# A graph attention layer: blocks of adj fetched in pairs, and fewer, larger transfers of x and of the results

## The chip, the cores and the metric

The kernel runs on one core of a Trainium2 chip. The metric is device time in microseconds (us) of one execution. Before the change it is 235.88 us, the median of three runs from 235.42 to 236.04. A core has five engines that run beside each other, each in its own program order: TensorE (PE, matmuls), VectorE (DVE), ScalarE (ACT), GpSimd (POOL) and SyncE (SP, which here only issues transfers). Sixteen DMA engines move data between the chip's memory (HBM) and the on-chip buffer (SBUF), 128 partitions wide.

## The reference

The layer takes x (4096 x 512), an additive mask adj (4096 x 4096), weights W (512 x 2048, four heads of 512) and vectors a, all f32:

```
ht  = (x @ W) per head                        # 4 heads, 4096 x 512
e   = leaky_relu(src[:, None] + dst[None, :], 0.01) + adj
att = softmax(e, axis=-1)
out = layernorm(x + mean over heads of (att @ ht))
```

The entries of adj go up to 1e9, while src and dst are small. So in nearly every row the softmax is 1 at the largest entry of adj and 0 elsewhere. The result of row i is then layernorm(x[i] + x[c] @ mean of W over heads), with c the column of the largest entry of adj[i].

## The kernel before

The kernel computes that short form, bounds for each row whether the lead of its largest entry is big enough, and runs a general path (`general`) for blocks of rows where it is not. The general path is not entered with these inputs.

The 4096 rows are worked on in 32 blocks of 128 rows; row p*32 + b stands in partition p of block b. So the same partition of two neighbouring blocks holds two neighbouring rows of adj. A block of adj is 2 MB, 16 KB in each partition. It lies in one of six buffers (`adj_pool`, AHEAD + 1). `hold` has room for all of x and becomes the result in place; its upper half first holds W.

The order on each engine is written out by hand. The loop over t = 0 to 31 (lines 423 to 477) does, at step t:

- SP issues the load of block t + 5 (`load_adj`, L122). It waits until DVE is through with block t - 1, which had the buffer. Before it, at t = 3, 7, 11, 15 and 19, SP issues x for four blocks (`load_x`, L125; 1 MB), at t = 26 x for the last four. Blocks 0 and 31 are fetched in four pieces, blocks 28 to 30 in two. SP has eight semaphores for its transfers, used in turn, so that at most eight are under way.
- DVE reduces block t to the maxima of segments (`segment_maxima`, L169): 16 entries each up to block 17, 32 from then on. It does it in two halves. Between them stands `find_column(t - 2)`: the second largest entry of the fetched segment (L208) and the place of the largest (L214). After both halves `find_segment(t)` finds the largest segment (L176, L178).
- POOL, in this order: adds up the column of block t - 2 (L216), issues the gather of the 128 rows of x that belong to it (`gather_rows`, `y`, L202), at even steps computes 1/sd for blocks t - 6 and t - 5 (`rstd`, L271 to L273), and for block t adds up the row of the segment (L185) and issues its fetch from adj (`lead`, `lead_early`, L191). Both gathers are indirect transfers, on another queue than SP's.
- PE transposes y of block t - 3 (`turn`, L229), adds x by a product with the identity (`residual`, L237) and multiplies with the mean of W (`products`, L244). Up to t = 14 it also turns W and forms vectors for the bound (L350, L358).
- ACT copies the transposed y (L231), takes the statistics of block t - 4 (`stats`, L266, L268), the norm of x (L251), and at even steps writes the normalised blocks t - 6 and t - 5 into `hold` (`finish`, L277).

From block 24 on (BEHIND) the sums are put aside into a buffer of adj (`put_by`) and finished in the tail, and x of those blocks is loaded at the last step. After the loop SP stores the results of blocks 0 to 23, blocks 0 to 7 in two transfers of four blocks, the others by two (`store`, L329). The tail (lines 486 to 542) looks for the column of the last block over the whole row (L222), gathers, multiplies and normalises the last blocks and stores them.

Of the kernel before, what the change touches and what calls it, by code (L numbers as in the profile page):

```python
# [9 lines left out]
F32 = mybir.dt.float32  # L10
# [10 lines left out]
P = 128  # L21
# [47 lines left out]
def leading_rows(ctx, tc, x, adj, W, a, out, ident, v, n_bad, any_bad):  # L69
# [8 lines left out]
    nc = tc.nc  # L78
    N, D = x.shape
    H = a.shape[0]  # L80
    KB, NB, S = D // P, N // P, N // E
    S_EARLY = N // E_EARLY
    AHEAD = 5
    Q = 4
    PIECES = 4
    LATE = NB - Q
    BEHIND = LATE - Q

    once = ctx.enter_context(tc.tile_pool(name="once", bufs=1))
    adj_pool = ctx.enter_context(tc.tile_pool(name="adj_pool", bufs=AHEAD + 1))  # L90
    y_pool = ctx.enter_context(tc.tile_pool(name="y_pool", bufs=4))
    lead_pool = ctx.enter_context(tc.tile_pool(name="lead_pool", bufs=2 * Q + 1))
    small = ctx.enter_context(tc.tile_pool(name="small", bufs=5))
    rows = ctx.enter_context(tc.tile_pool(name="rows", bufs=2))
    psum = ctx.enter_context(tc.tile_pool(name="psum", bufs=4, space=bass.MemoryType.PSUM))

    adj_rows = adj.rearrange("(p nb) m -> nb p m", nb=NB)
    adj_segs = adj.rearrange("n (s e) -> (n s) e", e=E)
    adj_segs_early = adj.rearrange("n (s e) -> (n s) e", e=E_EARLY)
    x_rows = x.rearrange("(p nb) d -> p nb d", nb=NB)  # L100
# [7 lines left out]
    w_sum = once.tile([P, KB, D], F32, name="w_sum")  # L108
    a_rows = once.tile([2 * H, D], F32, name="a_rows")

    once.tile([P, 32], F32, name="pad_end")
    adj_t = {}

    def pieces(ib):
        return PIECES if ib in (0, NB - 1) else 2 if ib >= LATE else 1

    def load_adj(ib):
        if 0 <= ib < NB:
            t = adj_t[ib] = adj_pool.tile([P, N], F32, name="adj_t")
            n = pieces(ib)  # L120
            for k in range(n):
                nc.sync.dma_start(t[:, ts(k, N // n)], adj_rows[ib][:, ts(k, N // n)])  # L122

    def load_x(lo, n):
        nc.sync.dma_start(hold[:, ds(lo, n), :], x_rows[:, ds(lo, n), :])  # L125
# [7 lines left out]
    for kb in range(KB):  # L133
        load_w(kb)
        load_adj(kb + 1)
    load_x(0, Q)
    for ib in range(KB + 1, AHEAD):
        load_adj(ib)

    make_identity(nc, ident)  # L140
    first = once.tile([P, NB], U32, name="first")
# [18 lines left out]
    seg_of, at_of, lead_of, y_t, yt_of, o_ps = {}, {}, {}, {}, {}, {}  # L160

    def segment_maxima(ib, lo, hi):

        e = E_EARLY if ib < EARLY else E
        if lo == 0:
            seg_of[ib] = small.tile([P, N // e], F32, name=f"seg{e}", bufs=2)
        n = max(pieces(ib), 2)
        for k in range(lo * n // PIECES, hi * n // PIECES):
            nc.vector.tensor_reduce(  # L169
                seg_of[ib][:, ts(k, N // e // n)],  # L170
                adj_t[ib][:, ts(k, N // n)].rearrange("p (s e) -> p s e", e=e), axis=AX.X, op=OP.max,
            )

    def find_segment(ib):
        seg = seg_of.pop(ib)
        nc.vector.max(out=top[:, ib, :], in_=seg)  # L176
        at = at_of[ib] = small.tile([P, 8], U32, name="at")
        nc.vector.max_index(at, top[:, ib, :], seg)  # L178
        if ib < NB - 1:
            fetch_segment(ib)  # L180
# [29 lines left out]
    def find_column(ib):  # L210
        if ib < BEHIND:
            find_inner(ib)
        within = small.tile([P, 8], U32, name="within")
        nc.vector.max_index(within, top[:, ib, :], lead_of[ib])  # L214
        col = small.tile([P, 1], U32, name="col")
        nc.gpsimd.tensor_tensor(col, at_of.pop(ib), within[:, 0:1], op=OP.add)  # L216
        gather_rows(ib, col)
# [31 lines left out]
    def row_norm(ib):  # L249
        sq = rows.tile([P, D], F32, name="sq")  # L250
        nc.scalar.activation(sq, hold[:, ib, :], AF.Square, accum_out=xx[:, ib : ib + 1])  # L251

    def put_by(ib):

        if ib == BEHIND:
            o_ps["by"] = adj_pool.tile([P, N // D, D], F32, name="adj_t")
        nc.scalar.copy(o_ps["by"][:, ib - BEHIND, :], o_ps.pop(ib))

    def add_x(engine, ib):
        o = o_ps[ib] = o_ps["by"][:, ib - BEHIND, :]  # L260
        engine.tensor_add(o, o, hold[:, ib, :])
# [8 lines left out]
    def rstd(i):  # L270
        nc.gpsimd.tensor_scalar(sd[:, i], sd[:, i], 1.0 / D, EPS, op0=OP.mult, op1=OP.add)  # L271
        nc.gpsimd.tensor_tensor(sd[:, i], sd[:, i], power[:, : i.stop - i.start], op=OP.pow)  # L272
        nc.gpsimd.tensor_mul(nm[:, i], nm[:, i], sd[:, i])  # L273
# [54 lines left out]
    def store(queue, lo, n):  # L328
        queue.dma_start(out_rows[:, ds(lo, n), :], hold[:, ds(lo, n), :])  # L329

    def mean_of_heads(kb):
        o = psum.tile([P, D], F32, name="o")
        for h in range(H):
            nc.tensor.matmul(o, ident, hold[:, w_at + kb * H + h, :], start=(h == 0), stop=(h == H - 1))  # L334
        nc.scalar.activation(w_sum[:, kb, :], o, AF.Copy, scale=1.0 / H)  # L335
# [5 lines left out]
    def turn_a():  # L341
        tp = psum.tile([P, KB, P], F32, name="tp", bufs=2)
        for k in range(KB):
            nc.tensor.transpose(tp[:, k, : 2 * H], a_rows[:, ts(k, P)], ident[: 2 * H, : 2 * H])
        nc.scalar.copy(at_d, tp[:, :, : 2 * H])

    def turn_w(kb, h):
        tp = psum.tile([P, KB, P], F32, name="tp", bufs=2)
        for k in range(KB):
            nc.tensor.transpose(tp[:, k, :], hold[:, w_at + kb * H + h, ts(k, P)], ident)  # L350
        wt = rows.tile([P, KB, P], F32, name="wt")
        nc.scalar.copy(wt, tp)  # L352
        return wt
# [9 lines left out]
    def head_norms():  # L363
        nc.vector.tensor_copy(v, pv)
        vv = once.tile([P, KB, 2 * H], F32, name="vv")
        nc.vector.tensor_mul(vv, v, v)
        pn = psum.tile([P, KB, 2 * H], F32, name="px", bufs=1)
        nc.tensor.matmul(pn, ones, vv, start=True, stop=True)
        n2 = once.tile([P, 2 * H], F32, name="n2")
        nc.vector.tensor_reduce(n2, pn.rearrange("p k c -> p c k"), axis=AX.X, op=OP.add)  # L370
        nc.scalar.activation(n2, n2, AF.Sqrt)
        both = once.tile([P, H], F32, name="both")
        nc.vector.tensor_add(both, n2[:, :H], n2[:, H:])
        nc.vector.tensor_reduce(vn, both, axis=AX.X, op=OP.max)
# [40 lines left out]
        nc.vector.tensor_reduce(total, pg, axis=AX.X, op=OP.add)  # L415
        nc.vector.tensor_scalar(any_bad, total, -1.0, float(N), op0=OP.mult, op1=OP.add)

    x_at = {lo - 1: (lo, Q) for lo in range(Q, BEHIND, Q)}
    vectors = [(kb, h) for kb in range(KB) for h in range(H)]
    vectors_at = {t: 2 if t < 3 else 1 for t in range(1, 15)}  # L420
    COLUMN, PROJECT, STATS, FINISH = 2, 3, 4, 6
# [1 line left out]
    for t in range(NB):  # L423
        if t == NB // 2:
            tc.mark_branch_hint_location("general", engines=HINTED)
        if t in x_at:
            load_x(*x_at[t])
        if t + AHEAD == NB - 1:
            load_x(LATE, Q)
        load_adj(t + AHEAD)  # L430
        middle = 1 if t == NB - 1 else 2
        segment_maxima(t, 0, middle)
        if t >= COLUMN:
            find_column(t - COLUMN)
        segment_maxima(t, middle, PIECES)
        pair = FINISH <= t < BEHIND + FINISH and t % 2 == 0
        if pair:
            rstd(slice(t - FINISH, t - FINISH + 2))
        if t == NB - 1:
            for ib in (BEHIND, BEHIND + 2):  # L440
                load_x(ib, 2)
        find_segment(t)
        if t < 2:
            mean_of_heads(t)
        elif t == 2:
            mean_of_heads(2)
            mean_of_heads(3)
        if t == 0:
            turn_a()
        turned = [(*vectors[0], turn_w(*vectors.pop(0))) for _ in range(vectors_at.get(t, 0))]  # L450
        if t == 16:
            head_norms()
        ib = t - PROJECT
        if t == NB - 1:
            for late in range(LATE, NB):
                row_norm(late)
        if t == NB - 2:
            residual(LATE)
            residual(LATE + 1)
        if ib >= 0:  # L460
            turn(ib)
            if ib > BEHIND:
                products(ib - 1, KB - 1, KB)
            if ib < BEHIND:
                residual(ib)
        for some in turned:
            head_vector(*some)
        if ib >= 0:
            products(ib, 0, KB if ib < BEHIND else KB - 1)
        if t >= BEHIND + STATS:  # L470
            put_by(t - STATS)
        elif t >= STATS:
            stats(t - STATS)
            row_norm(t - STATS)
        if pair:
            finish(t - FINISH)
            finish(t - FINISH + 1)
# [3 lines left out]
    nc.scalar.activation(xx, xx, AF.Sqrt)  # L481
    for ib in range(0, 2 * Q, Q):
        store(nc.sync, ib, Q)
    for ib in range(2 * Q, BEHIND, 2):
        store(nc.sync, ib, 2)
    add_x(nc.gpsimd, BEHIND)
    find_column(NB - 2)
    fetch_segment(NB - 1)
# [207 lines left out]
```

## Time and profile before

| what | value |
|---|---|
| median of three runs | 235.88 us |
| the profiled execution's own time | 236.22 us |
| its span, first to last instruction | 234.7 us |
| DVE busy | 192.2 us, 82% |
| PE busy | 200.7 us, 86% |
| ACT busy | 111.7 us, 48% |
| POOL busy | 100.7 us, 43% |
| moved by DMA | 97.06 MB, mean 414 GB/s |
| largest group: segment maxima, DVE L169 | 145.9 us in 68 |
| DVE idle before L169, released by the landing of adj | 29.4 us |
| mean granted PE clock | 0.959 |

The page divides the span into 40 slices of 5.87 us and gives the busy share of each engine in tenths. "DMA" is the mean share of the 16 DMA engines. Queue q1 carries SP's transfers, q0 the gathers. In the timeline each row has start, duration, engine, line, operation, output and input tile, and in brackets how long the engine was idle before it and what ended the wait. The page also has a chain, which follows the last work back to what released it; its share for the landing of adj is 42%.

### The profile page before, as it was taken

How to read it: one execution, taken by the hardware profiler on the slowest of the kernel's cores; microseconds unless marked ns; L12 is line 12 of the kernel's file. 1: busy time of each engine (PE TensorE's matmuls, PEld its weight loads, DVE VectorE, ACT ScalarE, POOL GpSimd, SP SyncE). 2: the span in 40 equal slices, each digit the busy share in tenths (PEclk: the TensorE clock that was granted, in tenths of full speed). 3: DMA queues.
4: the chain of work that ended last, by engine and by line, in shares of the span. 5: the costliest groups of instructions: out<-in, count | busy, mean ns of one | idle time of the engine just before them, and what ended most of it. 6: DMA issues, size and time to landing. Idle time of an engine off the chain costs nothing.

```text
span 234.7 us, 2494 instructions
## 1 busy us (share of the span) xinstructions
PE 200.7 (86%) x683; PEld 103.0 (44%) x683; DVE 192.2 (82%) x302; ACT 111.7 (48%) x267; POOL 100.7 (43%) x212
## 2 busy tenths in 40 slices
PE   0099859999999999999969979789987988999980
PEld 0034514765656555555525424244433442444360
DVE  2726975669969996999689998998699999989871
ACT  2002112255574647474747464646464555187561
POOL 2022142414626463546444555564364554457400
PEclk9999877999999999999997999979997999999998
DMA  6999999999999999999999999999999999999994
GB/s 233 423 409 430 431 429 415 430 426 425 431 431 421 426 428 428 438 418 436 421 437 431 419 434 422 434 417 435 422 436 413 422 426 423 413 425 420 414 374 197
DMA packets 13697, 97.06 MB, mean 414 GB/s; under 512 B 2152, under 2 KB 2664, under 8 KB 7792
## 3 DMA queue, kind: packets, MB, share of 16 engines
q1 hardware_dynamic: 10080, 88.08, 89.0%
q0 software_dynamic: 3584, 8.77, 9.5%
q8 instruction: 6, 0.10, 0.2%
q14 instruction: 11, 0.09, 0.1%
q10 hardware_dynamic: 16, 0.02, 0.0%
HBM read 88.47 MB, written 8.39 MB: 413 GB/s over the span
## 4 chain that ended last, share of the span: by engine, by line
DMA 48%; POOL 19%; issue 17%; DVE 11%; PE 2%; ACT 0%; POOLq 0%; SPq 0%; DVEq 0%
DMA adj_t<-in_adj_dram 42%; DVE seg L169 8%; POOL y L202 6%; POOL lead L191 5%; DMA y<-in_x_dram,col 3%; DMA lead<-in_adj_dram,row 2%; POOL sd L272 2%; PE o L286 2%; DVE col L222 1%; POOL row L185 1%; POOL start L198 1%; POOL col L216 1%; POOL lead_early L191 1%; DVE at L178 1%; DVE top L176 1%
## 5 line engine op out<-in xcount | busy, mean ns | idle before, releaser
L169 DVE TENSOR_REDUCE seg<-adj_t 128x128 f32<-128x2048 f32 (+3 forms) x68 | 145.9, 2148 | 29.5 <-DMA adj_t<-in_adj_dram 29.4
L244 PE MATMUL o<-w_sum,yt 128*128 128x512 f32 x248 | 116.8, 612 | 0.7 <-ACT yt L231 0.7
L244 PEld LDWEIGHTS o<-w_sum,yt 128*128 128x128 f32 x248 | 45.6, 195 | 55.7 <-issue 44.4
L231 ACT COPY yt<-tp 128x512 f32<-128x512 f32 x32 | 18.8, 588 | 44.4 <-PE tp L229 44.3
L202 POOL DMA_INDIRECT y<-in_x_dram,col x32 | 30.9, 964 | 16.5 <-POOL col L216 15.8
L334 PE MATMUL o<-hold,ident 128*128 128x512 f32 x32 | 21.1, 822 | 15.1 <-POOL row L185 11.5
L237 PE MATMUL o<-hold,ident 128*128 128x512 f32 x52 | 29.0, 645 | 0.0
L229 PE MATMUL tp<-ident,y 128*128 128x128 f32 x128 | 20.0, 280 | 9.2 <-DMA y<-in_x_dram,col 9.1
L185 POOL TENSOR_TENSOR row<-at,first 128x1 uint32<-128x1 uint32 x32 | 6.1, 190 | 43.9 <-DVE at L178 43.6
L229 PEld LDWEIGHTS tp<-ident,y 128*128 128x128 f32 x128 | 14.8, 142 | 21.9 <-issue 20.3
L352 ACT COPY wt<-tp 128x512 f32<-128x512 f32 x16 | 9.2, 587 | 31.5 <-PE tp L350 31.5
L191 POOL DMA_INDIRECT lead_early<-in_adj_dram,row x18 | 18.2, 1010 | 8.8 <-POOL row L185 8.8
L216 POOL TENSOR_TENSOR col<-start,within 128x1 uint32<-128x1 uint32 x31 | 5.9, 189 | 36.5 <-DVE within L214 36.5
L251 ACT ACTIVATE sq<-hold 128x512 f32<-128x512 f32 x32 | 19.8, 619 | 0.0
L358 PEld LDWEIGHTS pv<-at_d,wt 128*128 128x128 f32 x128 | 16.3, 191 | 6.8 <-ACT wt L352 3.7
L334 PEld LDWEIGHTS o<-hold,ident 128*128 128x128 f32 x32 | 8.0, 260 | 25.7 <-POOL row L185 11.5
L335 ACT ACTIVATE w_sum<-o 128x512 f32<-128x512 f32 x4 | 2.4, 598 | 33.6 <-PE o L334 33.6
L277 ACT ACTIVATE hold<-o,nm,sd 128x512 f32<-128x512 f32 x24 | 17.2, 771 | 0.0
L191 POOL DMA_INDIRECT lead<-in_adj_dram,row x14 | 14.1, 1006 | 6.9 <-POOL row L185 6.9
L268 ACT ACTIVATE sq<-o,nm 128x512 f32<-128x512 f32 x24 | 16.5, 688 | 0.8
L358 PE MATMUL pv<-at_d,wt 128*128 128x2 f32 x128 | 15.3, 244 | 0.6 <-ACT wt L352 0.6
L266 ACT ACTIVATE sq<-o 128x512 f32<-128x512 f32 x24 | 14.6, 608 | 0.0
(91 smaller groups left out, 151.4 us busy)
## 6 DMA issues: line engine op xcount, KB each, us to landing
adj_t<-in_adj_dram SPq DMA_DIRECT2D x27, 2048.0 KB
hold<-in_x_dram SPq DMA_DIRECT2D x7, 1024.0 KB
adj_t<-in_adj_dram SPq DMA_DIRECT2D x6, 1024.0 KB
out_dram<-hold SPq DMA_DIRECT2D x10, 512.0 KB
adj_t<-in_adj_dram SPq DMA_DIRECT2D x8, 512.0 KB
hold<-in_L_gnn_W_dram SPq DMA_DIRECT2D x4, 1024.0 KB
out_dram<-hold SPq DMA_DIRECT2D x2, 1024.0 KB
hold<-in_x_dram SPq DMA_DIRECT2D x2, 512.0 KB
```

The lines of the kernel that those rows point to most:

```text
L169: nc.vector.tensor_reduce(seg_of[ib][:, ts(k, N // e // n)], adj_t[ib][:, ts(k, N // n)].rearrange("p (s e) -> p s e", e=e), axis=AX.X, op ...
L191: nc.gpsimd.indirect_dma_start(out=lead, out_offset=None, in_=adj_segs_early if early else adj_segs, in_offset=bass.IndirectOffsetOnAxis(a ...
L202: nc.gpsimd.indirect_dma_start(out=y, out_offset=None, in_=x, in_offset=bass.IndirectOffsetOnAxis(ap=col[:, :1], axis=0),)
L229: nc.tensor.transpose(tp[:, kb, :], y[:, ts(kb, P)], ident)
L231: nc.scalar.copy(yt, tp)
L237: nc.tensor.matmul(o_ps[ib], ident, hold[:, ib, :], start=start, stop=False)
L244: nc.tensor.matmul(o_ps[ib], yt_of[ib][:, kb, :], w_sum[:, kb, :], start=(start and kb == 0), stop=(kb == KB - 1),)
L251: nc.scalar.activation(sq, hold[:, ib, :], AF.Square, accum_out=xx[:, ib : ib + 1])
L268: nc.scalar.activation(sq, o, AF.Square, bias=nm[:, i], accum_out=sd[:, i])
L277: nc.scalar.activation(hold[:, ib, :], o_ps.pop(ib), AF.Identity, bias=nm[:, i], scale=sd[:, i])
L334: nc.tensor.matmul(o, ident, hold[:, w_at + kb * H + h, :], start=(h == 0), stop=(h == H - 1))
L358: nc.tensor.matmul(pv[:, kb, h : 2 * H : H], wt[:, k, :], at_d[:, k, h : 2 * H : H], start=(k == 0), stop=(k == KB - 1),)
```

## The change

- The six buffers become one tile, `ring`, with six slots; block b has slot b % 6.
- Blocks 4 to 15 are fetched by two: one transfer of 4 MB into two neighbouring slots, 32 KB in a row in each partition on both sides. The first pair is issued ahead of the loop, the others at t = 2, 4, 6, 8 and 10, when both slots are free. Both blocks have the same landing.
- Block 0 is fetched in one transfer; DVE reduces it in two halves instead of four quarters.
- x comes for blocks 4 to 11 at t = 3, for 12 to 15 at t = 11 and for 16 to 23 at t = 15: two transfers of 2 MB and one of 1 MB for five of 1 MB.
- The results of blocks 16 to 23 are stored in two transfers of 1 MB instead of four of 0.5 MB.

SP issues 57 transfers instead of 70. The order of PE, ACT and POOL and, but for block 0, of DVE stays as it was.

```diff
+    SLOTS = AHEAD + 1
+    PAIRED = range(4, 16)
...
-    adj_pool = ctx.enter_context(tc.tile_pool(name="adj_pool", bufs=AHEAD + 1))
...
+    adj_pairs = adj.rearrange("(p nb) m -> p nb m", nb=NB)
...
+    ring = once.tile([P, SLOTS, N], F32, name="adj_t")
...
     def pieces(ib):
-        return PIECES if ib in (0, NB - 1) else 2 if ib >= LATE else 1
+        return PIECES if ib == NB - 1 else 2 if ib >= LATE else 1
+
+    def load_pair(ib):
+        slot = ib % SLOTS
+        for k in range(2):
+            adj_t[ib + k] = ring[:, slot + k, :]
+        nc.sync.dma_start(ring[:, ds(slot, 2), :], adj_pairs[:, ds(ib, 2), :])

     def load_adj(ib):
-        if 0 <= ib < NB:
-            t = adj_t[ib] = adj_pool.tile([P, N], F32, name="adj_t")
+        if 0 <= ib < NB and ib not in PAIRED:
+            t = adj_t[ib] = ring[:, ib % SLOTS, :]
...
     load_x(0, Q)
-    for ib in range(KB + 1, AHEAD):
-        load_adj(ib)
+    load_pair(PAIRED[0])
...
-            o_ps["by"] = adj_pool.tile([P, N // D, D], F32, name="adj_t")
+            o_ps["by"] = ring[:, (ib + 2) % SLOTS, :].rearrange("p (b d) -> p b d", d=D)
...
-    x_at = {lo - 1: (lo, Q) for lo in range(Q, BEHIND, Q)}
+    x_at = {Q - 1: (Q, 2 * Q), 3 * Q - 1: (3 * Q, Q), 4 * Q - 1: (4 * Q, 2 * Q)}
...
-        load_adj(t + AHEAD)
+        if t + AHEAD in PAIRED[2:]:
+            if t % 2 == 0:
+                load_pair(t + AHEAD - 1)
+        else:
+            load_adj(t + AHEAD)
...
-    for ib in range(2 * Q, BEHIND, 2):
+    for ib in range(2 * Q, 4 * Q, 2):
         store(nc.sync, ib, 2)
+    for ib in range(4 * Q, BEHIND, Q):
+        store(nc.sync, ib, Q)
```

## The prediction

> **What bounds the kernel now.** I read the page's slices first, then the chain, then the timeline of VectorE (DVE) around the blocks whose fetching changes, then the groups by tile of the two gathers, then the timelines of GpSimd (POOL), ScalarE (ACT) and TensorE (PE) around one step.
>
> The page's rows of slices, queues and chain:
>
> ```profile
> DMA  6999999999999999999999999999999999999994
> GB/s 233 423 409 430 431 429 415 430 426 425 431 431 421 426 428 428 438 418 436 421 437 431 419 434 422 434 417 435 422 436 413 422 426 423 413 425 420 414 374 197
> q1 hardware_dynamic: 10080, 88.08, 89.0%
> q0 software_dynamic: 3584, 8.77, 9.5%
> DMA 48%; POOL 19%; issue 17%; DVE 11%; PE 2%; ACT 0%; POOLq 0%; SPq 0%; DVEq 0%
> ```
>
> The DMA engines are full from the first to the last slice but one, at about 428 GB/s. SP's transfers are queue q1, GpSimd's gathers queue q0. The chain changes between DMA, DVE and POOL: several limits lie close together. How close, the timeline of DVE shows (start, duration, idle before and its releaser); these are the first reductions of blocks 8, 9, 10, 12, 16, 24 and 27:
>
> ```profile
> 67.56 2.29 DVE L169 TENSOR_REDUCE seg<-adj_t 128x128 f32<-128x2048 f32 x1 [1.67 <-DMA adj_t<-in_adj_dram]
> 73.28 2.29 DVE L169 TENSOR_REDUCE seg<-adj_t 128x128 f32<-128x2048 f32 x1
> 78.95 2.27 DVE L169 TENSOR_REDUCE seg<-adj_t 128x128 f32<-128x2048 f32 x1
> ...
> 92.12 2.29 DVE L169 TENSOR_REDUCE seg<-adj_t 128x128 f32<-128x2048 f32 x1 [1.76 <-DMA adj_t<-in_adj_dram]
> ...
> 116.68 2.29 DVE L169 TENSOR_REDUCE seg<-adj_t 128x128 f32<-128x2048 f32 x1 [1.82 <-DMA adj_t<-in_adj_dram]
> ...
> 166.18 2.29 DVE L169 TENSOR_REDUCE seg<-adj_t 128x64 f32<-128x2048 f32 x1 [2.56 <-DMA adj_t<-in_adj_dram]
> ...
> 182.84 2.29 DVE L169 TENSOR_REDUCE seg<-adj_t 128x64 f32<-128x2048 f32 x1 [0.30 <-DMA adj_t<-in_adj_dram]
> ```
>
> DVE needs 5.66 us for a block (73.28 to 78.95) and waits once in four blocks, behind an x transfer, for 1.7 to 2.6 us. So DMA leads by under 2 us in about 24.5, and from block 27 on DVE never waits for adj again. Whatever DVE loses before block 27 beyond these waits arrives at the end.
>
> The groups of the two gathers, and rows of step 10 (block 10 in hand), of POOL, ACT and PE:
>
> ```profile
> DMA to landing us min/median/max: 5.3/5.8/6.4
> ...
> DMA to landing us min/median/max: 6.6/7.7/8.7
> ```
>
> ```profile
> 82.26 0.96 POOL L202 DMA_INDIRECT y<-in_x_dram,col  x1 [0.54 <-POOL col L216]
> 83.29 0.19 POOL L271 TENSOR_SCALAR sd<-sd 128x2 f32<-128x2 f32 x1
> 84.78 0.19 POOL L185 TENSOR_TENSOR row<-at,first 128x1 uint32<-128x1 uint32 x1 [0.21 <-DVE at L178]
> 85.49 1.06 POOL L191 DMA_INDIRECT lead_early<-in_adj_dram,row  x1 [0.52 <-POOL row L185]
> ...
> 82.22 0.19 ACT L268 ACTIVATION_READ_ACCUMULATOR sq<-o,nm 128x1 f32 x1
> ...
> 79.77 0.63 PE L229 MATMUL tp<-ident,y 128*128 128x128 f32 x4 [0.17 <-DMA y<-in_x_dram,col]
> ```
>
> The first landing line is of lead_early (up to block 17), the second of y. The lead fetch of block t goes out 0.79 us after DVE's search of t ended and is used 2.2 us into step t+2. Between search and use lie 7.81 us (73.33 to 81.14 for block 8), so a fetch may take about 6.9 us; a later landing stops DVE.
>
> **The change, part by part.**
>
> *Bytes saved on the queue.* All bytes stay. The trace's packet records show on q1 611 ns for a 16 KB packet, 309 for 8 KB, 159 for 4 KB, 9 for a semaphore write: some 9 ns of each packet are not bytes. I take 2x611-9 = 1213 ns for a 32 KB one. Per engine, pairing turns 12x8 packets into 48: 48x9 = 0.43 us less. Block 0 has 32x159 = 5.09 us of packets and gets 8x611 = 4.89: 0.20. The two doubled x loads go from 32x309 to 16x611: 0.11. Eleven transfers fewer ahead of the last block: 0.10. Together 0.84 us; the stores save 0.14 and two semaphores more, behind the last loads. That is all that DMA can give, since the queue never ran dry. The Trainium skill, page "DMA: Bandwidth & Descriptors", section "Anatomy of one DMA", gives each DMA about 2 us of fixed cost; by that 13 transfers fewer would be an estimate of 26 us saved. No slice of DMA here has room for it, as the next transfers are queued already.
>
> *Block 0 in one piece.* DVE's first reduction moves from 4.43 us to about 8.3, and block 0 ends near 14; block 1 lands only at 16.25, and DVE waits 5.1 us for it now. Cost nothing; without that wait it would cost 3 us.
>
> *Stores by four.* The same issue place behind the loads. Their packets of 8 KB instead of 4 may pass the last gather of y, issued at 216.13 and used at 223.47. y gathers beside 8 KB packets took 6.6 us, beside 4 KB 7.2 to 7.6 (y of blocks 27 and 31), so between -0.7 and +0.7 us; I take 0, since most of that gather should still run beside the 4 KB stores of blocks 8 to 15.
>
> *SP's order.* SP waits for two slots instead of one. When pair (10,11) is issued, (6,7), x and (8,9) are still queued, 16 us of work; later pairs have 11 or more. No DMA idles. Lane waits on SP get fewer. x for blocks 16 to 23 waits for PE's use of W, over by step 14.
>
> *Landing in pairs.* Block 4 lands with block 5, at 48.5 instead of 39.3. Blocks 8 and 9 come after a double x: 67.56, plus block 9 (8x611 = 4.9), plus the second half of x (2.5), less 0.5 already saved, is 74.4. DVE has finished block 7 by 72 and waits. From 74.4 on it has work up to block 27: pairs land at about 85.4, 96.4 and 107.4 (2x4.85 plus two gathers of y at 0.65 each), DVE is ready at 85.7, 97 and 108. Blocks 8 to 15 take 8x5.66 = 45.3 us; blocks 16 to 26 took 182.84-116.68 = 66.2, less waits of 0.8, 0.15, 0.2, 2.6 and 0.3, so 62.2 of work. DVE would begin block 27 at 74.4+45.3+62.2 = 181.9, in front of DMA (182.84-0.84 = 182.0). So pairing alone is paid for exactly, and all slack is spent.
>
> *Gathers beside 32 KB packets.* This is what I expect to decide. The semaphore records give the lead fetch 5.25 to 5.45 us beside 8 KB packets (blocks 25 to 28) and 5.8 to 6.8, mean 6.1, beside 16 KB. 0.8 us for 302 ns of packet: it waits out 2.65 packets. The y gather took 6.6 beside 8 KB, mean 8.2 beside 16 KB: 5.3 packets. No row shows 32 KB. Lower bound: nothing, if the queue cuts to 16 KB (then 6.1 and 8.2). The same slope gives 6.1+2.65x0.602 = 7.7 and 8.2+5.3x0.602 = 11.4. Upper: the slowest lead row, 6.8, is 4.9 packets, which gives 9.7, for single fetches. I take 7.7 and 11.4, as both steps from 8 to 16 KB fit whole packets being waited out. The same page's section "Queues, rings and completion order" says that an engine changes queue only after a whole packet, typically 9 to 17 descriptors; with 9 descriptors of 611 ns a wait would be 5.5 us, an estimate that the 0.8 us above contradicts: here about one descriptor passes per turn. Its direction speaks against this change.
>
> By steps: lead 8 goes out at 80.9 and lands at 88.6, wanted at 87.9: DVE stops 0.8 us in block 10. y of block 6 goes out at 77.7, lands at 89.1; PE turns it at 89.2, and ACT's statistics, 2.64 us after the turn (79.77 to 82.41), are ready at 91.9. POOL, in order, has issued y 8 by 90.8 and waits 1.1 us for them before line 271; behind it stands lead 10, which goes out at 93.9 instead of 93.1 and lands at 101.6. Block 12 wants it at 100.05: 1.65 us. Leads 9 and 11 gain from the stop before them, lead 12 flies after the last pair. Sum 0.8+1.65 = 2.45, all on DVE's path: block 27 at 184.35, 1.5 us later than 182.84. The tail after it is DVE's and the last gather's and moves along.
>
> Profiled execution: span 234.7, time 236.22; 236.2+1.5 = 237.7. It lay 0.34 above the median of 235.88, so the median becomes 237.4.
>
> **Rivals.** *Faster: the fetches do not wait longer* (packets cut, or another order of service). Then DVE is at the adj landing again, 0.84 us earlier from block 24 to the end: 235.0. For it: the slope from 4 to 8 KB is not there (lead 29 took 5.9 beside 4 KB). Against it: x rows of 8 KB, also merged from four rows of 2 KB, stand as single 8 KB packets, so a pair's two rows should merge too.
>
> *No measurable change: the stops are about 1 us.* The break-even is 182.84-181.9 = 0.94 us of stops; a lead of 7.2 us instead of 7.7 gives about that. 235.2 to 236.6.
>
> *Much slower: stops in every block.* Leads of 8.6 us or more, or y near 13, put POOL's wait at 2 to 3 us on each even step; 4 to 6 us of stops, 239 to 241. Blocks 16 to 27 have no slack left to return it. POOL's row at 84.78 waits for DVE, not for line 271, which speaks against so much.
>
> **How the numbers follow.** Stops between 1.7 and 4.2 us: 0.50, which is 236.6 to 239.1, with 237.4 the likeliest. More: 0.06. About 1 us: 0.17. No longer waits: 0.27. About 0.3%, 0.7 us, is what a measurement here can tell from no change. So faster 0.27, same 0.17, slower 0.56. The likeliest case's own range is 236.6 to 239.1; for 8 in 10 it must take in the faster case at 235.0 with its 0.2 of spread: 234.8 to 239.2.
>
> **What would show it.** q1 packets of 32 KB near 1213 ns between 40 and 108 us; lead_early landings up to 7.7 and y to 11 there; DVE waits of 0.5 to 2 us for lead in blocks 10 and 12, POOL waiting for ACT before line 271's successor; a DVE wait of about 2 us at block 8 and none for adj from 10 to 26. If DVE again waits for adj at block 24, the slack was larger than I count, and the faster rival holds. I am wrong in size if two rows are not merged, or if DMA yields more than 9 ns a packet.

## The result and the profile after

The changed kernel takes 246.78 us, the median of six runs from 245.93 to 249.07. The kernel before took 235.56 us in six runs beside it. The ratio is 1.0483, with a 95% interval of 1.0435 to 1.0530: 11.2 us slower, where 1.5 us slower was forecast. The direction was right; the size was not, and the time lies outside the range.

The profiled execution of the changed kernel took 245.93 us with a span of 244.4. These are its rows of slices and queues, and the shares of its chain:

```profile
DMA  6999999999999999999999999999999999997225
GB/s 252 429 429 416 432 467 412 429 430 438 426 455 411 432 443 408 387 430 435 422 424 428 433 424 430 433 426 430 421 415 428 424 418 423 418 426 305 88 109 198
q1 hardware_dynamic: 8208, 88.08, 85.1%
q0 software_dynamic: 3584, 8.77, 9.3%
DMA 27%; issue 24%; POOL 23%; DVE 16%; PE 8%; POOLq 0%; ACT 0%; SPq 0%; DVEq 0%
```

DMA was full to the last slice but one before. Now its last four slices have 7, 2, 2 and 5 tenths, which with slices of 6.1 us is some 15 us of idle: the transfers arrive in time and the engines are late. The share of DMA in the chain fell from 48% to 27%.

The list of DVE's waits gives the total in us, the number of waits and the longest. These are its first two rows:

```profile
DVE seg L177 <- DMA adj_t<-in_adj_dram: 25.5, 5, 11.8
DVE inner L216 <- DMA lead_early<-in_adj_dram,row: 14.0, 5, 3.6
```

The second row is the loss. DVE stood still for 14.0 us in five stops because the fetched segment of the block two steps back had not landed. The timeline of DVE shows where (start, duration, idle before and its releaser); the rows of L177 are the first reductions of blocks 4, 8, 16 and 27:

```profile
47.87 2.29 DVE L177 TENSOR_REDUCE seg<-adj_t 128x128 f32<-128x2048 f32 x1 [11.78 <-DMA adj_t<-in_adj_dram]
...
70.66 0.18 DVE L216 MAX8 inner<-lead_early 128x8 f32<-128x16 f32 x1 [3.58 <-DMA lead_early<-in_adj_dram,row]
74.55 2.27 DVE L177 TENSOR_REDUCE seg<-adj_t 128x128 f32<-128x2048 f32 x1
79.29 0.18 DVE L216 MAX8 inner<-lead_early 128x8 f32<-128x16 f32 x1 [2.47 <-DMA lead_early<-in_adj_dram,row]
87.18 0.18 DVE L216 MAX8 inner<-lead_early 128x8 f32<-128x16 f32 x1 [2.14 <-DMA lead_early<-in_adj_dram,row]
95.38 0.18 DVE L216 MAX8 inner<-lead_early 128x8 f32<-128x16 f32 x1 [2.44 <-DMA lead_early<-in_adj_dram,row]
104.53 0.18 DVE L216 MAX8 inner<-lead_early 128x8 f32<-128x16 f32 x1 [3.40 <-DMA lead_early<-in_adj_dram,row]
130.66 2.27 DVE L177 TENSOR_REDUCE seg<-adj_t 128x128 f32<-128x2048 f32 x1
193.55 2.27 DVE L177 TENSOR_REDUCE seg<-adj_t 128x64 f32<-128x2048 f32 x1
```

There is one stop in each of blocks 7 to 11, where the pairs are on their way, and no other for a lead_early. After block 4 DVE never waits for adj again: blocks 16 and 27, which waited 1.82 and 0.30 us before, begin without a wait, 14.0 and 10.7 us later than before. So a part of the loss was given back by the waits for DMA that are gone, and the rest went through to the end.

The groups by tile give the time from issue to landing, lead_early first and y second:

```profile
DMA to landing us min/median/max: 5.4/6.6/13.6
```
```profile
DMA to landing us min/median/max: 3.4/8.1/13.7
```

The longest lead fetch grew from 6.4 to 13.6 us, the longest y gather from 8.7 to 13.7. By the semaphore records the leads of blocks 5 to 9 took 10.6, 13.6, 11.3, 11.7 and 13.0 us, and y of blocks 3 to 7 took 11.4, 13.6, 12.9, 13.7 and 13.7.

The trace's packet records tell why. This is not a view of the profile but worked out of those records: the first start and the last end of the data packets of each gather on q0, over all 16 DMA engines. y t is always asked for some 3 us ahead of lead t+2.

```
before                       after
y 6      75.03 to  78.54     y 5      76.76 to  83.01
lead 8   78.41 to  79.78     lead 7   82.24 to  85.46
y 7      80.72 to  83.58     y 6      84.68 to  92.37
lead 9   83.93 to  84.43     lead 8   91.36 to  93.62
y 8      86.41 to  89.41     y 7      92.36 to 100.30
                             lead 9   96.61 to 102.93
                             y 8     100.58 to 105.69
```

Before, y and lead of a block move for about 4 us together (y of blocks 2 to 14 on average 3.1, lead of blocks 4 to 15 0.9), and then the gather queue moves nothing until the next. After, y moves for 6 to 8 us and the lead behind it for 2 to 6, and the queue has almost no pause in these rows, from 76.8 to 102.9 us (in the records of all gathers from 60.9 to 106.3). Its starts of y are 7.9, 7.7 and 8.2 us apart. That is DVE's new period: blocks 8, 9 and 10 took 8.22, 7.89 and 8.20 us instead of 5.66.

### The profile page after: what moved, and what is told of

Same layout as the page of the kernel before. It is cut to its first block, busy times and chain, and to the rows that moved or that the text cites. A ratio compares the mean times of both kernels' runs of the same rounds, so it can differ in the third digit from the quotient of the medians.

```text
span 244.4 us, 2470 instructions
## 1 busy us (share of the span) xinstructions
PE 203.7 (83%) x683; PEld 105.1 (43%) x683; DVE 191.1 (78%) x300; ACT 112.0 (46%) x267; POOL 100.6 (41%) x212
## 4 chain that ended last, share of the span: by engine, by line
DMA 27%; issue 24%; POOL 23%; DVE 16%; PE 8%; POOLq 0%; ACT 0%; SPq 0%; DVEq 0%
DMA adj_t<-in_adj_dram 15%; DVE seg L177 12%; POOL y L210 7%; DMA lead_early<-in_adj_dram,row 5%; POOL lead L199 5%; PE o L252 5%; DMA hold<-in_L_gnn_W_dram 4%; DMA y<-in_x_dram,col 3%; POOL lead_early L199 3%; POOL sd L280 2%; POOL row L193 2%; POOL start L206 2%; POOL col L224 2%; PE o L294 1%; DVE at L186 1%
## 5 line engine op out<-in xcount | busy, mean ns | idle before, releaser
L177 DVE TENSOR_REDUCE seg<-adj_t 128x128 f32<-128x2048 f32 (+2 forms) x66 | 145.2, 2205 | 25.5 <-DMA adj_t<-in_adj_dram 25.5
L252 PE MATMUL o<-w_sum,yt 128*128 128x512 f32 x248 | 118.9, 622 | 0.7 <-ACT yt L239 0.7
L252 PEld LDWEIGHTS o<-w_sum,yt 128*128 128x128 f32 x248 | 46.1, 198 | 56.1 <-issue 45.8
L237 PE MATMUL tp<-ident,y 128*128 128x128 f32 x128 | 20.7, 287 | 17.8 <-DMA y<-in_x_dram,col 17.7
L342 PE MATMUL o<-hold,ident 128*128 128x512 f32 x32 | 19.4, 762 | 16.1 <-DMA hold<-in_L_gnn_W_dram 16.1
L245 PE MATMUL o<-hold,ident 128*128 128x512 f32 x52 | 29.1, 647 | 0.0
L366 PEld LDWEIGHTS pv<-at_d,wt 128*128 128x128 f32 x128 | 18.1, 209 | 7.9 <-issue 3.9
L342 PEld LDWEIGHTS o<-hold,ident 128*128 128x128 f32 x32 | 7.4, 243 | 25.6 <-issue 19.4
L366 PE MATMUL pv<-at_d,wt 128*128 128x2 f32 x128 | 16.8, 255 | 0.6 <-ACT wt L360 0.6
## 6 DMA issues: line engine op xcount, KB each, us to landing
hold<-in_L_gnn_W_dram SPq DMA_DIRECT2D x4, 1024.0 KB, 12.6
```

The lines of the kernel that those rows point to most:

```text
L177: nc.vector.tensor_reduce(seg_of[ib][:, ts(k, N // e // n)], adj_t[ib][:, ts(k, N // n)].rearrange("p (s e) -> p s e", e=e), axis=AX.X, op ...
L237: nc.tensor.transpose(tp[:, kb, :], y[:, ts(kb, P)], ident)
L245: nc.tensor.matmul(o_ps[ib], ident, hold[:, ib, :], start=start, stop=False)
L252: nc.tensor.matmul(o_ps[ib], yt_of[ib][:, kb, :], w_sum[:, kb, :], start=(start and kb == 0), stop=(kb == KB - 1),)
L366: nc.tensor.matmul(pv[:, kb, h : 2 * H : H], wt[:, k, :], at_d[:, k, h : 2 * H : H], start=(k == 0), stop=(k == KB - 1),)
```

## The experiments

The leading theory is that the larger packets slow the gather queue. Its rivals are that the landing in pairs, the doubled x or one of the smaller edits costs the time, and, within the theory, that it is a delay and not a rate. Where the experiments say "y" and "lead", the gathers above are meant.

**1. Pairs in packets of 16 KB.** The six slots are made 64 B longer, so that the two rows of a pair no longer lie in a row in SBUF.

```diff
-    ring = once.tile([P, SLOTS, N], F32, name="adj_t")
+    ring = once.tile([P, SLOTS, N + 16], F32, name="adj_t")[:, :, :N]
```

> The change as it is, but each slot of the ring is 64 bytes longer, so that a pair's two rows no longer lie in one piece: the same 57 transfers and the same common landings, in packets of 16 KB. Theory A (32 KB packets hold the gathers, and the lead fetch also stands behind the y gather on queue q0): lead fetches back to 5.8 to 6.8 us, no stop of DVE for a lead over 0.5 us, time 234.7 to 236.0. Rival B (the common landing of two blocks itself spends DVE's slack): stops move to adj, time 238 or more.

Measured: 238.42 us, ratio 1.0102 (1.0069 to 1.0136). The first rows of DVE's waits, and one further down:

```profile
DVE seg L177 <- DMA adj_t<-in_adj_dram: 29.5, 6, 11.6
DVE n L378 <- PE px L376: 2.3, 1, 2.3
...
DVE inner L216 <- DMA lead_early<-in_adj_dram,row: 0.8, 2, 0.6
```

The stops for the lead fell from 14.0 to 0.8 us and no early lead took longer than 7.5. With the same pairs, the same landing and the same x, most of the loss is gone. So the packets of 32 KB make most of it. But 1% is left, with a wait of 2.3 us for PE that was 0.6 before: the time lies above the range of theory A and in that of rival B, so the run shows that the packets are not all of it.

**2. Pairs alone.** Packets of 32 KB; block 0, x and the stores as before.

```diff
-        return PIECES if ib == NB - 1 else 2 if ib >= LATE else 1
+        return PIECES if ib in (0, NB - 1) else 2 if ib >= LATE else 1
...
-    x_at = {Q - 1: (Q, 2 * Q), 3 * Q - 1: (3 * Q, Q), 4 * Q - 1: (4 * Q, 2 * Q)}
+    x_at = {lo - 1: (lo, Q) for lo in range(Q, BEHIND, Q)}
...
-    for ib in range(2 * Q, 4 * Q, 2):
+    for ib in range(2 * Q, BEHIND, 2):
         store(nc.sync, ib, 2)
-    for ib in range(4 * Q, BEHIND, Q):
-        store(nc.sync, ib, Q)
```

> Only the pairs: block 0 in four pieces, x by four blocks, stores by two as before. Theory A: the 32 KB packets alone do it, lead fetches of 10 us and more in five blocks, time 244 to 249. Rival C (the double x transfers and the earlier x take part): under 241.

Measured: 243.54 us, ratio 1.0325 (1.0286 to 1.0364), with 12.6 us of stops for the lead in five. The time lies just under theory A's range. The pairs by themselves bring most of the loss; by the two ratios the rest of the change adds 1.6% of the time before, some 3.7 us.

**3. Everything but the pairs.** Block 0 whole, x and the stores as in the change, blocks 4 to 15 one by one.

```diff
-    PAIRED = range(4, 16)
+    PAIRED = range(0)
...
-    load_pair(PAIRED[0])
```

> Everything but the pairs: block 0 whole, x and stores in larger transfers, blocks 4 to 15 one by one. Theory A: no 32 KB packet, so 234.8 to 235.6, 0.4 us less work on the queue. Rival C: 238 or more, by the later landing of blocks 8 to 11 behind the double x.

Measured: 235.68 us, ratio 0.9994 (0.9975 to 1.0013). Seven transfers fewer on the full queue change nothing that can be measured. The doubled x makes DVE wait longer at block 8 (69.56 us instead of 67.56), the wait for PE grows to 2.3 us here too, and two leads stop DVE for 2.8 us. Yet none of it reaches the end: after block 8 DVE waits for adj only once more, for 0.2 us at the last block, and it begins block 27 at 181.77, 1.1 us earlier than before. So the slack that DVE had at blocks 12 to 24 pays for it. The chain is now 44% DMA and 32% PE, where it was 48% and 2%: DMA alone no longer sets the time.

**4. y away from the queue of the gathers.** y of blocks 1 to 9 is replaced by the block's own rows of x, loaded through ACT's queue. So these blocks add the wrong rows.

```diff
+        if ib in range(1, 10):
+            nc.scalar.dma_start(y, x_rows[:, ib, :])
+            return
         nc.gpsimd.indirect_dma_start(
```

> The change, but for blocks 1 to 9 y is not gathered: ACT's queue loads as many rows of x in order, so these blocks' products are of other rows. Queue q0 then carries the lead fetches alone while the 32 KB packets pass. Theory A: what made a lead 11 to 13 us was the y gather in front of it on the same queue; alone it takes 7 to 8.5 us, stops of DVE sum to 1 to 4 us, time 236.5 to 240. Rival D (a single small fetch itself waits for six 32 KB packets and more): leads stay at 10.5 us or more, stops at 8 us or more, time 243 or more.

Measured: 251.12 us, ratio 1.0646. The latency came as expected: the leads of blocks 6 to 9, with the same 32 KB packets on q1 but no y ahead of them, took 7.3, 7.9, 7.7 and 7.2 us. The time did not. DVE stopped for leads for 13.8 us all the same, since these now went out 2.9 to 6.7 us after their search instead of 0.8. A row of POOL's timeline shows why:

```profile
84.23 0.19 POOL L282 TENSOR_SCALAR sd<-sd 128x2 f32<-128x2 f32 x1 [7.42 <-ACT sq L279]
```

POOL waits 7.4 us for ACT's statistics in `rstd`, with the lead behind it. ACT was late because PE was: PE waited 4.5 us, up to 81.03, for y of block 4, which ACT had issued at 66.22. So the loads of y had become slow themselves, from 9.6 to 19.5 us where the landing is recorded. The run puts a new wait in the place of the old one. It settles the lead's own latency beside 32 KB packets, and nothing about the time.

**5. Pairs of 16 KB with x by four.** Experiment 1 with x as before.

```diff
-    ring = once.tile([P, SLOTS, N], F32, name="adj_t")
+    ring = once.tile([P, SLOTS, N + 16], F32, name="adj_t")[:, :, :N]
...
-    x_at = {Q - 1: (Q, 2 * Q), 3 * Q - 1: (3 * Q, Q), 4 * Q - 1: (4 * Q, 2 * Q)}
+    x_at = {lo - 1: (lo, Q) for lo in range(Q, BEHIND, Q)}
```

> Pairs in packets of 16 KB as in the first experiment, and x by four blocks as before; block 0 whole and the stores by four stay. The first experiment (16 KB pairs with the doubled x) took 238.4 us and began block 8 at 74.97 and block 27 at 186.07. Theory A, the doubled x is what made that rest: block 8 then begins near 72.0 (67.56 of the kernel before, plus 4.9 for block 9, less 0.5), block 12 near 96.5, block 27 at 182 to 183, and the time is 235.0 to 236.0. Theory B, the landing in pairs alone costs it: after the pause for a pair DVE takes blocks without a pause, and what stands in the way then is PE and ACT, which let POOL's lead fetches go out 1 to 3 us late; block 27 at 184 to 186, time 236.8 to 238.2.

Measured: 238.09 us, ratio 1.0100 (1.0086 to 1.0115). Blocks 8 and 12 began at 72.18 and 97.03 as theory A has it, block 27 only at 184.27, and the time is that of theory B. But neither theory named what the packet records then showed: in this kernel the 16 KB packets took 622 ns on average, in the kernel before 612 and in experiment 6 on the same chip 614. With 224 of them to each DMA engine that is some 2 us of a full queue. In experiment 1 it was 622 as well. The longer slots, a means of the experiment, had a price of their own; runs 9 to 12 deal with it.

**6. Only block 0 whole and the stores by four.** No pairs, x by four.

```diff
-    PAIRED = range(4, 16)
+    PAIRED = range(0)
...
-    load_pair(PAIRED[0])
...
-    x_at = {Q - 1: (Q, 2 * Q), 3 * Q - 1: (3 * Q, Q), 4 * Q - 1: (4 * Q, 2 * Q)}
+    x_at = {lo - 1: (lo, Q) for lo in range(Q, BEHIND, Q)}
```

> No pairs, x by four blocks as before; only block 0 whole and the stores by four. By the packets this saves 0.2 us of the full queue (block 0) and something behind the loads. Theory A (the queue's time decides, DVE waits in every four blocks): 235.2 to 235.7, ratio 0.997 to 1.001. Theory B (the stores by four disturb the last gathers of y, or block 0 whole puts DVE behind): 236.0 to 237.0. DVE's wait for adj at block 8 is back at 1.5 to 2 us, where the doubled x made it 4.9.

Measured: 235.56 us, ratio 0.9992 (0.9983 to 1.0000). Theory A. These two edits cost nothing and gain at most 0.2%. No version that ran and does the whole work is measurably faster than the kernel before.

**7. The change without y.** y of blocks 1 to 9 is not gathered; PE turns the block's own rows of x out of `hold`. This leaves out the bytes of nine gathers, and these blocks add the wrong rows. The packets of 32 KB stay.

```diff
     def gather_rows(ib, col):
+        if ib in range(1, 10):
+            y_t[ib] = hold[:, ib, :]
+            return
```

> The change, with the gathers of y of blocks 1 to 9 left out: the rows of x of the block itself are turned in their place, so the bytes of nine gathers (nine times some 0.6 us of the full queue) are left out as well. The pairs keep packets of 32 KB. In the changed kernel the queue of gathers is nearly without a pause from 84.7 to 102.9 us: y moves for 6 to 8 us, the lead behind it for 2 to 3.6 us, 8 to 11 us together, against 5.66 us of DVE for a block. Theory A (y and lead share one queue, whose service beside 32 KB packets takes longer than DVE's block): leads of blocks 6 to 9 land 7 to 8 us after their issue, DVE stops for them 0.5 to 3.5 us in all instead of 14, block 27 at 180.5 to 184, time 234.0 to 237.5. Rival (a lead's own latency beside 32 KB is 10 us or more): stops of 10 us or more, time above 243.

Measured: 236.45 us, ratio 0.9975 (0.9932 to 1.0019). The six executions spread from 233.25 to 236.93 us, which is why the median and the ratio point to different sides of no change. The landing times of lead_early, then a row of DVE's timeline, the only stop for lead_early that is left:

```profile
DMA to landing us min/median/max: 6.5/7.0/7.6
```
```profile
85.71 0.18 DVE L219 MAX8 inner<-lead_early 128x8 f32<-128x16 f32 x1 [0.46 <-DMA lead_early<-in_adj_dram,row]
```

Packets of 32 KB alone do not make a lead late; with y in the same queue they do. Theory A holds. The nine gathers left out also save q0 5.8 us of DMA time (nine times 0.64 us of packets), so the time itself is not to be compared to the last microsecond. The view of landings counts only some of the fetches; by the semaphore records the leads of blocks 5 to 9 took 6.7 to 7.7 us, and the longest of all, block 3's, 8.0.

**8. The lead first.** All bytes and packets of the change. In steps 4 to 16 the search of block t and its lead fetch come ahead of the column and the y of block t - 2 and of `rstd`. A lead then has two whole steps until its use.

```diff
+    LEAD_FIRST = range(4, 17)
...
-        if t >= COLUMN:
+        if t >= COLUMN and t not in LEAD_FIRST:
             find_column(t - COLUMN)
...
-        if pair:
+        if pair and t not in LEAD_FIRST:
             rstd(slice(t - FINISH, t - FINISH + 2))
...
         find_segment(t)
+        if t in LEAD_FIRST:
+            find_column(t - COLUMN)
+            if pair:
+                rstd(slice(t - FINISH, t - FINISH + 2))
```

> The change, with another order in steps 4 to 16: the search of block t and its lead fetch come first, then the column and the y gather of block t-2 and rstd. A lead then has 10.5 to 11 us from its issue to its use instead of 6.9, and is issued in front of y, not behind it. All bytes and packets stay. Theory O (only the delay counts: a lead that stands behind y is late for its use): leads that take up to 11 us are in time, DVE stops 0 to 3 us for them in all, block 27 at 182 to 185, time 235 to 238. Theory Q (the rate counts: beside 32 KB packets the queue of gathers needs 8 to 10 us for y and lead of a block, so DVE can't take blocks faster, however early they are asked for): the stops are put off by some us, but blocks 8 to 12 still take 7.5 to 9 us each, block 27 at 188 to 193, time 240 to 246.

Measured: 249.25 us, ratio 1.0576 (1.0533 to 1.0618), slower than the change. By the packet records y 4, 5, 6 and 7 begin to move at 74.89, 82.81, 91.61 and 99.85 us, 7.9, 8.8 and 8.2 us apart, as in the change, with the leads in between and no pause. The timeline of DVE has the stops for leads that are left and two waits for PE:

```profile
93.27 0.18 DVE L216 MAX8 inner<-lead_early 128x8 f32<-128x16 f32 x1 [2.94 <-DMA lead_early<-in_adj_dram,row]
101.63 0.18 DVE L216 MAX8 inner<-lead_early 128x8 f32<-128x16 f32 x1 [2.60 <-DMA lead_early<-in_adj_dram,row]
131.94 0.19 DVE L372 COPY v<-pv 128x32 f32<-128x32 f32 x1 [1.70 <-PE pv L366]
140.43 0.19 DVE L378 TENSOR_REDUCE n<-px 128x8 f32<-128x32 f32 x1 [8.08 <-PE px L376]
```

The stops for leads are down from 14.0 to 5.5 us, yet blocks 10 and 11 take 8.70 and 8.36 us. y now lands up to 18 us after its issue, PE gets it late, and DVE pays 8.1 us at step 16 for what PE has not done. That speaks for theory Q: the queue gives out y and lead of one block in about 8.3 us, in this order of asking as in the other. Theory Q was not right in all: blocks 8, 9 and 12 took 5.7 to 5.8 us, not 7.5 to 9, and its forecast of the time, 240 to 246, was too low, chiefly by the wait for PE.

**9 and 10. Pairs split over slots three apart**, a second way to 16 KB packets, with x by four (9) and as in the change (10).

```diff
+    halves = ring.rearrange("p (h k) n -> p h k n", h=2)
+
+    def slot_of(ib):
+        return ib // 2 % 3 + 3 * (ib % 2)
+
     def load_pair(ib):
-        slot = ib % SLOTS
         for k in range(2):
-            adj_t[ib + k] = ring[:, slot + k, :]
-        nc.sync.dma_start(ring[:, ds(slot, 2), :], adj_pairs[:, ds(ib, 2), :])
+            adj_t[ib + k] = ring[:, slot_of(ib + k), :]
+        nc.sync.dma_start(halves[:, :, slot_of(ib), :], adj_pairs[:, ds(ib, 2), :])
```

> As the fifth experiment (pairs in packets of 16 KB, x by four blocks, block 0 whole, stores by four), but the two blocks of a pair go to slots three apart instead of to slots that are 64 B longer. In the fifth run all packets of 16 KB took 622 ns on average where the kernel before shows 612; some 224 of them to each engine make 2.2 us, and its 8 KB packets were slower too. Theory A, the longer slots made that run slow and not the pairs: packets of 16 KB at 611 to 613 ns, block 27 at 181.7 to 183, time 235.3 to 236.4. Theory B, two rows in one transfer cost it: packets near 620 ns again, block 27 near 184, time 237.3 to 238.3.

> The change with the two blocks of a pair in slots three apart: packets of 16 KB and slots of the old length, all else as in the change. It parts the change's 11 us cleanly: what is above this run is the packets of 32 KB. Theory A (the first experiment's 238.4 us held some 1.7 us of its longer slots): packets of 16 KB at 611 to 613 ns, block 8 at 74.0 to 74.7, block 16 at 119.5 to 120.5, block 27 at 183.5 to 185, time 236.3 to 237.3, so 9.5 to 10.5 us of the loss are the 32 KB packets. Theory B (as the first experiment): 238.0 to 239.0, and the packets take 8 to 9 us. Theory C (my prediction's sum without its stops, pairs paid for exactly): 235.0 to 235.7.

Measured: 302.21 and 303.40 us, ratios 1.2815 and 1.2865. All theories missed. DVE's first wait row of run 9, and SP's:

```profile
DVE seg L181 <- DMA adj_t<-in_adj_dram: 96.2, 7, 31.1
```
```profile
SPq L128 <- DVE seg L181: 121.0, 5, 33.7
```

SP held the pair loads until DVE was through with blocks in other slots, and DVE waited up to 31 us for loads: block 1, long on its way, began at 45.1, about when the first pair can have landed. A transfer into slots k and k+3 seems to have been ordered as if it wrote all that lies between them. That is inferred from the waits alone and stays open; the runs say nothing on the question they were made for.

**11 and 12. Slots 512 B longer** instead of 64 B, with x by four (11) and as in the change (12).

```diff
-    ring = once.tile([P, SLOTS, N], F32, name="adj_t")
+    ring = once.tile([P, SLOTS, N + 128], F32, name="adj_t")[:, :, :N]
```

> As the fifth experiment (pairs in packets of 16 KB, x by four blocks, block 0 whole, stores by four), with slots 512 B longer instead of 64 B. There the 16 KB packets took 622 ns on average, in the kernel before 612, about 2.2 us to each engine in all. Theory A, the place of the slots made them slow: with 512 B they take 611 to 613 ns, block 27 begins at 181.7 to 183, time 235.3 to 236.4. Theory B, two rows in one transfer make them slow: 620 ns or more again, block 27 near 184, time 237.3 to 238.3.

> The change in packets of 16 KB, with slots 512 B longer; all else as in the change. Theory A: packets of 16 KB at 611 to 613 ns, block 8 at 74.0 to 74.7, block 27 at 183.5 to 185, time 236.3 to 237.3, so that 9.5 to 10.5 of the change's 11 us are the 32 KB packets. Theory B (as the first experiment, slots 64 B longer): 238.0 to 239.0. Theory C (the prediction's sum without its stops, pairs paid for exactly): 235.0 to 235.7.

Measured: 237.16 us (1.0038, 1.0011 to 1.0066) and 237.43 us (1.0069, 1.0049 to 1.0089). The 16 KB packets took 615 and 614 ns on average with a median of 611: near theory A's 611 to 613, and not theory B's 620. Run 12 lies 0.1 us above theory A's range. Between it and the change stand the packets of 32 KB and the 512 B between the slots: 4.1% of the time by the two ratios, 9.8 us (8.5 to 11.0, if their errors are independent). The other 0.7%, some 1.6 us, are left for the landing in pairs, the doubled x and whatever the longer slots cost; no run parts these. Run 11 fell into two groups, four runs at 235.3 to 235.5 and eight at 236.8 to 238.1. Its profile is of the lower group and has block 27 at 181.87; what makes the upper one stays open. The kernel before shows such a spread beside it, 235.2 to 237.0 us.

Run 12's profile is of its slowest execution, 238.87 us. What is left in it shows in a table by stage. The columns are the length of the stretch, then busy time and number of instructions of PE, PE's weight loads, DVE, ACT and POOL, then the granted PE clock, the DMA share and GB/s. The kernel before, blocks 8 to 11 and 12 to 15, and then run 12, the same blocks:

```profile
67.56:92.12 24.56, 24.39 (x106) 14.42 (x105) 22.25 (x33) 14.94 (x37) 12.96 (x27) 1.00 1.01 427
92.12:116.68 24.56, 24.56 (x106) 14.47 (x104) 22.19 (x33) 15.20 (x37) 12.52 (x27) 1.00 1.01 426
```
```profile
74.49:97.15 22.66, 22.66 (x102) 13.86 (x101) 22.11 (x33) 13.45 (x35) 11.03 (x23) 1.00 1.01 427
97.15:119.81 22.66, 22.66 (x99) 13.38 (x97) 22.11 (x33) 13.33 (x33) 12.24 (x26) 1.00 1.01 427
```

PE was already busy for all of these stretches before. Its timeline shows its own pace: these two rows are the first product of two neighbouring blocks in the kernel before, and PE does not pause between them.

```profile
97.98 0.60 PE L229 MATMUL tp<-ident,y 128*128 128x128 f32 x4
104.04 0.60 PE L229 MATMUL tp<-ident,y 128*128 128x128 f32 x4
```

PE needs 6.06 us for a block here, and 6.06 in run 12 too, where DVE needs 5.66. When DVE hurries through these stretches without its waits, 22.66 us for four blocks instead of 24.56, PE falls behind by 0.4 us with each block and gets less done in each stretch (102 and 99 instructions instead of 106). What it owes is asked for at step 16, where DVE needs the vectors for the bound:

```profile
DVE n L378 <- PE px L376: 2.0, 1, 2.0
```

That wait was 0.6 us before, and block 16 took 9.92 us instead of 7.38. A stop of 1.0 us for a lead is in it too: POOL issued that lead late, behind a wait for ACT's statistics.

## Why the prediction was wrong in size

**Bytes, packets, block 0, stores, SP: right.** The 32 KB packets have a median of 1213 ns, as estimated. q1's packet time fell from 208.92 to 207.95 us per engine, 0.97 for an expected 0.98 with the stores. That the two agree so closely is luck, since the average packets moved as well: those of 16 KB from 612 to 616 ns, those of 4 KB from 163 to 160. Block 1 began at 15.70, earlier than before, so block 0 whole costs nothing. DMA did not run dry before 220 us. Experiments 3 and 6 give 0.9994 and 0.9992 for these edits. The section that the prediction quotes gives its fixed cost for transfers that GpSimd issues; taken for SP's as well, seven transfers fewer would be an estimate of 14 us, of which nothing shows in experiment 3.

**Landing in pairs: the place right, "paid for exactly" wrong.** Block 4 began at 47.87 and block 8 at 74.55, against 48.5 and 74.4. Block 8 came right because its wait for the pair and the first stop, 3.58 us in block 7, fell together. "From 74.4 on it has work up to block 27" counted DVE alone. PE was full from block 8 to block 16 and needed 48.1 us for eight blocks (75.78 to 123.83 in run 12) where the sum has 45.3, so DVE's slack there could not be spent freely. Run 12 prices the step at some 1.6 us, where the prediction had zero. In the change itself this did not bind: the stops gave PE its time, and block 16 took 7.36 us.

**Gathers beside 32 KB packets: the cause right, the working wrong.** This is the step that failed: "By steps: lead 8 goes out at 80.9 and lands at 88.6". It adds to each gather the latency that it would have by itself; lead 8 went out at 83.65 and took 11.7 us. (From its own rounded times the two stops are 0.7 and 1.55 us, 2.25 in all and not 2.45; that changes nothing here.) For a lead without a y ahead of it 7.7 us was right (7.2 to 7.9 in experiment 4, 6.7 to 8.0 in experiment 7). For y 11.4 was right for the gathers that found the queue empty (11.3 for block 1, 11.4 for block 3). But y and lead stand in one queue, and the table of packet records shows them moving one behind the other in the order of their issue. The prediction never asked how much of them the queue can serve in 5.66 us. The records for that were there: y and lead moved for 4.0 us of each 5.66. While a y moved, 3.4 to 5.2 packets of 16 KB passed on each engine before, 4.1 on average, and 4.1 to 6.1 of 32 KB after, 5.0 on average: about one for each of y's four packets or a little more. So the count of packets waited out changes little and the time goes mainly with their size: twice 4.0 us is 8.0, more than DVE's block. From there on the queue sets the pace. Five blocks at 8.0 instead of 5.66 us would have been 11.7 us of stops; 14.0 were measured, 2.45 predicted.

The page "DMA: Bandwidth & Descriptors" of the Trainium skill, section "Queues, rings and completion order", says that an engine changes queue only after a packet of typically 9 to 17 descriptors. With 9 descriptors of 1.2 us, each turn of SP's queue would last an estimated 11 us, and 44 us would go by if there were a turn for each of the four packets that a y has on an engine. A y moved for 6 to 8 us in all, with 4.1 to 6.1 descriptors of 32 KB beside it. The direction of the rule holds here, its count does not.

**The sum by blocks.** Block 27 was forecast at 184.35 and began at 193.55, 9.2 us later. Block 8 gives 0.15 of it. From block 8 to block 12 there are 33.47 us, which is 22.64 of work and 10.83 of stops and small delays: 8.4 more than the 2.45. Blocks 12 to 15 take 22.64 us, as forecast. From block 16 to 27 there are 62.9 for 62.2, which gives 0.7. The profiled execution was forecast at 237.7; those 9.2 us on it make 246.9, and it took 245.93. So the tail behind block 27, which was to move along, took 1.0 us less (50.9 us to the end of the span instead of 51.9). The median of 246.78 lies 9.4 above the 237.4 of the forecast.

**POOL's wait for ACT: did not occur.** `rstd` was to wait 1.1 us at step 10. The timeline of POOL in that step:

```profile
96.51 0.96 POOL L210 DMA_INDIRECT y<-in_x_dram,col  x1 [0.54 <-POOL col L224]
97.54 0.19 POOL L279 TENSOR_SCALAR sd<-sd 128x2 f32<-128x2 f32 x1
...
99.74 1.06 POOL L199 DMA_INDIRECT lead_early<-in_adj_dram,row  x1 [0.52 <-POOL row L193]
```

L279 follows the y issue at once, and the lead goes out 3.2 us behind y, as before. The stops had put all of DVE's and POOL's steps off, and so the statistics were in time. The wait did turn up in runs without long stops, for another reason than the prediction's: in run 12 it was 0.58, 1.37 and 2.15 us at steps 10, 12 and 14, in experiment 1 0.93, 1.73 and 2.24. It grows by some 0.8 us in two blocks, as PE falls behind DVE by 0.4 us in each.

**The rivals.** "Stops in every block" was the case that came, in five blocks in a row, at 0.06 and priced at 239 to 241. It was put down because POOL's row waited for DVE and not for `rstd`. That row tells of POOL; the limit was in the queue that POOL fills, on which the prediction shows no row but the landing times. The faster rival fell with the trace of the change: the packets were not cut, and the fetches waited longer.

## What to carry to other kernels

In this kernel a small gather paid for the size of the packets that another queue had on the same DMA engines: larger transfers on the full queue gained at most a microsecond of packet time and cost ten in the gathers. For a queue in order, work out its rate first (what all its gathers of one step need together, against the step) and only then the latency of one; once the rate was short here, asking for the lead earlier did not help. And slack is to be counted on every engine of the stage: DVE's waits for DMA were not all free time, since PE needed 6.06 us for a block beneath them and DVE 5.66.

## What was not expected of the hardware

Slots 64 B longer than 16 KB made the 16 KB packets into them slower, 622 ns on average, where slots without a gap showed 612 to 616 (runs 9 and 10, whose loads were held up, apart: 628 and 633) and slots 512 B longer 614 to 615. On a queue without a pause that was about 1 us at the end (238.42 us for 237.43, 238.09 for 237.16), though the intervals of the first two ratios overlap and the runs were on different chips. And the wait of a small packet goes by packets of the other queue more than by bytes: while the four packets of a y moved, 4.1 of 16 KB passed on average, and 5.0 of 32 KB.
